# An attention block on one core: group statistics on VectorE in two parts, v's bias placed elsewhere, the weighted sums' banks as two tiles, v's sums in place

## The chip, the cores and the metric

The kernel runs on one core of one Trainium2 chip. The metric is the device time of one execution in microseconds (us). The core has a matrix engine (PE in the profile; its weight loads are listed apart, as PEld), a vector engine (DVE), a scalar engine (ACT), GpSimd (POOL) and a sync engine (SP) that issues transfers. Each engine works through its own queue in order and waits at an instruction until what it needs is done. Matrix products are written to PSUM, which has banks of 128 x 512 fp32 elements; the other tiles are in SBUF, 128 partitions wide.

## The reference

The input is a batch of B = 16 images with C = 512 channels and N = 32 x 32 = 1024 positions, all in fp32. For each image:

```
xn  = group_norm(x, 8 groups of 64 channels) * gamma + beta
q, k, v = qkv_w @ xn + qkv_b              # each 512 x 1024; 4 heads of 128 channels
p   = softmax(q_head^T k_head / sqrt(128))   # 1024 x 1024 per head
o   = p v^T per head, put together to 512 x 1024
y   = x + proj_w @ o + proj_b
```

The channels lie on the partitions, 128 to a tile. So a group of 64 channels is one half of a tile's partitions, two blocks ("quadrants") of 32 partitions. A bias of v adds a constant per channel to v, and, since the weights of a softmax sum to one, the same constant to o.

## The kernel before

The work on an image is a pipeline over "heads". While the attention of image b, head h runs (8 steps, one for each block of 128 keys), other work is put between its matmuls by `plan_head` (L1059):

- head 0: the second half of q and k of image b;
- head 1: the projection of image b-1 (`proj_groups`, L795), and of image b+1 the loads, the statistics (`stats_chunk`, `stats_group`) and the normalisation;
- head 2: the first half of q and k of image b+1;
- head 3: v of image b+1 (`v_groups`, L754).

Image 0's own q, k and v are made before, in an opening part; its v comes from `v_units` (L722). In image 0, head 1 there is no projection yet; there the sums of the projection's weights are made and stored in DRAM (`kept_group`, L943; the sums on DVE at L428 to L442), from which `w<-kept` loads them, and q, k and v's weights likewise.

**Attention.** In each step, `scores` makes two halves s of the scores (L844, PE), ACT makes p = exp(s) (L850), DVE adds the p's into tot (L858), and one step later `weighted_sum` adds p times v into the PSUM tile po (L912, PE). po is one tile of two banks, from a pool with one buffer, so a head's two halves are two banks of one tile. After the last step each half is copied to SBUF (`o`, L919, ACT), and in the next head `divide` multiplies o by the inverse of the sums (L922, DVE).

**Projections.** q, k, v and proj are matrix products by a two-level Strassen scheme (`two_levels`, L521; `strassen`, L470). For each group of outer products, seven inner products (L604, PE) go into two alternating PSUM banks, called x and y; DVE makes the sums of the inputs (L572) and of the products (L628, tensor_add from a bank and an SBUF tile into a row of a tile R), and ACT copies some banks (L484, L626). The last inner product accumulates into bank y, after the L628 of the sum c22 (`v_r<-v_y,v_u` for v) has read y. L677 adds whole R tiles to each other.

**v's end.** For images 1 to 15 `finish` (L758 on) takes two rows a and c of R tiles and adds them into a new tile vt from the pool `ypool` (L766, DVE), transposes vt in blocks of 32 x 32 into a tile vu of the same pool (L769, DVE), and sends vu through DRAM (`vd`) into the final layout with transfers issued by POOL. `ypool` has 4 buffers.

**Statistics.** For image b+1 `stats_chunk` makes sum and sum of squares of each tile of 128 channels on ACT. `stats_group` then takes the averages over the 64 channels of a group by `Norm.group_steps`: a copy (L82), a matmul with an averaging matrix into a bank of the y buffers (pm, L83), three small DVE operations, a copy, a second matmul (pv, L88), an addition of epsilon (L89) and the power -1/2 on POOL (L90). `scale` and `shift` (L76, L100, L102) give two columns per channel, which `normalise` applies on ACT (L109).

**Biases.** In the fast path v gets no bias. Instead `bias_of_v` (L929), planned in image 0's head 1, adds proj_w times v's bias to the projection's bias: 16 matmuls of one column, in four groups of four, and four small additions on DVE. Each matmul here, as all in fp32, is two passes on PE.

**What sets the order.** Each engine's order is made by a scheduler from the order in which the program issues the instructions, from `tc.high_priority(URGENT)`, and from `tc.issue_after(...)`, which puts instructions behind a named other one (the statistics stand behind `added[b-1, 1, n]`, which is the L858 of step n of head 1). Around these points, a changed or removed instruction can change the place of others too.

A second, slower function (`general_path`) is in the program behind a branch, and is not taken with these inputs.

Of the kernel before, what the change touches and what calls it, by code (L numbers as in the profile page):

```python
# [10 lines left out]
F32 = mybir.dt.float32  # L11
# [5 lines left out]
P = 128  # L17
HEADS = 4
# [168 lines left out]
def fast_path(ctx, tc, x, sources, out, consts, flag, dims):  # L187
# [35 lines left out]
    ones = one.tile([BLK, 1], F32, name="ones")  # L223
    xs, xb, vs, qs, ks, os_, ob = {}, {}, {}, {}, {}, {}, {}
# [23 lines left out]
    nc.vector.memset(neghalf, -0.5)  # L248
    for t, src in (
        (gamma_sb, gamma), (beta_sb, beta), (qkb_sb, qk_b), (vb_sb, v_b), (projb_sb, proj_b)  # L250
    ):
        nc.gpsimd.dma_start(t, src)
# [3 lines left out]
    def stats_chunk(b, c):  # L256
        if c == 0:
            mvs[b] = gn.tile([P, NCC, 2], F32, tag="mv", name=f"mv_{b}")
# [4 lines left out]
        nc.scalar.mul(mvs[b][:, c, 0:1], sums[:, 0:1], 1.0 / N)  # L263
        nc.scalar.mul(sums[:, 1:2], sums[:, 0:1], -1.0 / N)
        nc.scalar.activation(
            junk, xs[b, c], AF.Square, bias=sums[:, 1:2], accum_out=sums[:, 2:3]
        )
        nc.scalar.mul(mvs[b][:, c, 1:2], sums[:, 2:3], 1.0 / N)

    def stats_group(b):  # L270


        g = []

        def part(n, first, last):
            if not g:
                g.extend(norm.group_steps(mvs[b]))
            with tc.issue_after(added[b - 1, 1, n].ins), tc.high_priority(URGENT):
                for step in g[first:last]:
                    step()  # L280

        def scale():
            n = 4 if b > 1 else 3
            part(n, 9, 10)
            with tc.issue_after(added[b - 1, 1, n].ins), tc.high_priority(URGENT):
                mu, sc = norm.result
                sh = norm.shift(mu, sc)
            for c in range(NCC):
                scaled[b, c] = sc, sh, c

        return [lambda: part(2, 0, 6), lambda: part(3, 6, 9), scale]
# [462 lines left out]
    def v_groups(b):  # L754
# [3 lines left out]
        def finish(which, h, a, c):  # L758
            pair, half = int(which[1]) - 1, int(which[2]) - 1
            if (b, pair) not in vs:  # L760
# [4 lines left out]
            t = ypool.tile([P, HALF], F32, tag="y", name=f"vt_{b}_{pair}_{h}_{half}")  # L765
            nc.vector.tensor_add(t, a, c)  # L766
# [4 lines left out]
                t.rearrange("p (j q i) -> p j q i", q=n, i=BLK),  # L771
# [135 lines left out]
    def weighted_sum(s, half):  # L907
        b, h, j = where(s)
        if j == 0 and half == 0:
            po[b, h] = ps_o.tile([P, N], F32, tag="o", name=f"po_{b}_{h}")  # L910
        i = ts(half, HALF)
        nc.tensor.matmul(  # L912
            po[b, h][:, i], v_block(b, h, j), ps[s][:, i],
            start=(j == 0), stop=(j == NB - 1),
        )
        if j == NB - 1:
            if (b, h) not in os_:
                os_[b, h] = opool.tile([P, N], F32, tag="o", name=f"o_{b}_{h}")
            last_eviction[b] = nc.scalar.copy(os_[b, h][:, i], po[b, h][:, i])  # L919

    def divide(b, h):
        nc.vector.tensor_mul(os_[b, h], os_[b, h], rinv.pop((b, h)))  # L922

# [4 lines left out]

    def bias_of_v(o):  # L929

        acc = ps_a.tile([P, HALF], F32, tag="y", name=f"pb_{o}")
        half, r = divmod(o, 2)
        for c in range(NCC):
            block = stage["proj"][f"a{half + 1}{c // KC + 1}"]
            nc.tensor.matmul(
                acc[:, 0:1], block[:, ts(r * KC + c % KC, P)], vb_sb[:, c : c + 1],
                start=(c == 0), stop=(c == NCC - 1),
            )
        nc.vector.tensor_add(
            projb_sb[:, o : o + 1], projb_sb[:, o : o + 1], acc[:, 0:1]  # L940
        )
# [117 lines left out]
    def plan_head(b, h):  # L1059
# [9 lines left out]
        elif h == 1:  # L1069
# [4 lines left out]
            else:  # L1074
                plan[0].append(lambda: load_x(b + 1))
                spread(plan, [lambda c=c: stats_chunk(b + 1, c) for c in range(NCC)], 2, 4)
                sums, power, scale = stats_group(b + 1)
                if b == 0:

                    plan[4] += [sums, power, scale]  # L1080
                else:
                    plan[4].insert(0, sums)
                    plan[4].insert((len(plan[4]) + 1) // 2, power)
                    plan[5].insert(0, scale)
# [7 lines left out]
            if b == 0:  # L1092
                for g in range(len(OUTER)):
                    plan[g // 2].append(lambda g=g: kept_group("v", g))
                    plan[NB // 2 - 1 + g].append(lambda g=g: kept_group("proj", g))
                plan[2].append(lambda: stage_blocks("proj"))
                spread(plan, [lambda o=o: bias_of_v(o) for o in range(NCC)], 3, 5)
# [113 lines left out]
    for s in range(steps + 1):  # L1211
# [12 lines left out]
        for half in range(NH2):  # L1224
            if s < steps:
# [4 lines left out]
                if half == 1 and j == 4 and s > NB:  # L1230

                    with tc.issue_after(added[b, h, 4].ins):
                        divide(*where(s - NB)[:2])
            if s > 0:
                weighted_sum(s - 1, half)
# [11 lines left out]
def general_path(ctx, tc, x, sources, out, consts, dims):  # L1247
# [26 lines left out]
    with tc.For_i(0, B, 1) as b:  # L1274
# [16 lines left out]
        for h in range(HEADS):  # L1291
# [9 lines left out]
            for qb in range(NB):  # L1301
# [27 lines left out]
                nc.scalar.copy(o[h][:, ts(qb, P)], acc[:, :P])  # L1329
# [46 lines left out]
```

## Time and profile before

| | |
|---|---|
| Time, median of 3 runs | 3169.58 us (3167.83 to 3171.18) |
| Profiled execution: time / span | 3171.08 us / 3169.30 us |
| Busy: PE, DVE, ACT, POOL | 3156.8 (100%), 2635.8 (83%), 1438.3 (45%), 516.3 (16%) us |
| Chain that ended last | PE 96%, DVE 2%, DMA 1% |
| Granted clock of PE | 1.0 of full speed |
| L83, pm matmuls of 4 columns | 30 passes, 4.3 us |
| L88, pv matmuls of 4 columns | 30 passes, 5.8 us |
| L935, bias of v | 32 passes, 3.8 us |
| L766, v's sums on 512 columns | 90 instructions, 711 ns each |
| L769, v's transposes | 120 instructions, 1131 ns each |
| L922, division | 63 instructions, 1226 ns each |

A line of a group of the profile names the line of the kernel, the engine, the operation, out<-in by the program's names, and the shape; then the busy time in us, the mean of one in ns, and the idle time of the engine ahead of it with what ended it. A line of a timeline has the start in us from the beginning of the span, the duration, and then the same names; "x2" is two instructions in a row, and in brackets stands how long the engine was idle before and for what. Instructions that follow each other overlap by about 0.1 us, so the distance between starts ("step") is shorter than a duration, and for matmuls much shorter. A line of the chain has start, length and what the time was spent in.

### The profile page before, as it was taken

Reading aid. Unit: us, or ns where it says so; the run is one execution under the profiler, and the core shown is the slowest. Engines: PE = TensorE matmul, PEld = TensorE weight load, DVE = VectorE, ACT = ScalarE, POOL = GpSimd, SP = SyncE. Lnnn points to the kernel's source line nnn. Section 1 sums busy time; section 2 is a strip of 40 time slices with the busy share of each in tenths; the row PEclk is TensorE's granted clock in tenths of the full one; section 3 lists DMA queues with packets and bytes.
Section 4 is the critical chain, followed back from the end, with each engine's and each line's share of the span. In section 5 each row is a group of like instructions: output and inputs, shape, how many; then the busy total and the mean of one; then the engine's idle time right before and its main releaser. Section 6 shows DMA issues by size and latency. Waiting matters only on the chain.

```text
span 3169.3 us, 34227 instructions
## 1 busy us (share of the span) xinstructions
PE 3156.8 (100%) x10502; PEld 2188.2 (69%) x10502; DVE 2635.8 (83%) x4642; ACT 1438.3 (45%) x2711; POOL 516.3 (16%) x896
## 2 busy tenths in 40 slices
PE   9999999999999999999999999999999999999999
PEld 7566676677776776767767667677676776766664
DVE  9878879788897888878888787987879978788785
ACT  3535435354353443535435454453534545344333
POOL 0011221111211112211122111222012221122200
PEclk9999999999999999999999999999999999999999
DMA  5554554545545555454554545555455564555531
GB/s 176 186 190 154 187 173 152 173 152 194 168 164 163 155 184 176 167 165 144 193 173 159 170 144 192 167 174 171 144 177 170 176 187 133 178 158 187 180 119 48
DMA packets 210668, 524.83 MB, mean 166 GB/s; under 512 B 32176, under 2 KB 65456, under 8 KB 210480
## 3 DMA queue, kind: packets, MB, share of 16 engines
q1 hardware_dynamic: 133088, 282.39, 28.6%
q0 software_dynamic: 64000, 204.54, 19.3%
q10 hardware_dynamic: 13392, 35.66, 3.5%
q8 instruction: 86, 1.41, 0.2%
q14 instruction: 102, 0.84, 0.1%
HBM read 389.30 MB, written 133.17 MB: 165 GB/s over the span
## 4 chain that ended last, share of the span: by engine, by line
PE 96%; DVE 2%; DMA 1%; issue 0%; SPq 0%; POOL 0%; ACT 0%; ACTq 0%; DVEq 0%
PE s L844 27%; PE po L912 27%; PE qk_x L604 12%; PE qk_y L604 9%; PE pp_x L604 6%; PE v_x L604 6%; PE v_y L604 4%; PE pp_y L604 4%; PE lx L999 0%; DVE qk_t L572 0%; DMA x<-in_x 0%; PE ly L999 0%; DVE tot L858 0%; DVE qk_r L628 0%; DVE qk L712 0%
## 5 line engine op out<-in xcount | busy, mean ns | idle before, releaser
L912 PE MATMUL po<-p,v 128*128 128x512 f32 x2048 | 1049.4, 594 | 0.7 <-ACT p L850 0.7
L850 ACT ACTIVATE p<-s 128x512 f32<-128x512 f32 x1024 | 610.6, 596 | 963.7 <-PE s L844 960.0
L844 PE MATMUL s<-qk,qk 128*128 128x512 f32 x2048 | 1047.4, 593 | 0.3 <-DVE qk L712 0.3
L912 PEld LDWEIGHTS po<-p,v 128*128 128x128 f32 x2048 | 603.6, 302 | 322.7 <-issue 214.5
L858 DVE TENSOR_TENSOR tot<-tot,p 128x1024 f32<-128x1024 f32 x385 | 470.2, 1221 | 158.1 <-ACT p L850 156.1
L844 PEld LDWEIGHTS s<-qk,qk 128*128 128x128 f32 x2048 | 387.7, 190 | 88.6 <-issue 29.9
L604 PEld LDWEIGHTS qk_x<-qk_t,w 128*128 128x128 f32 x1344 | 251.8, 190 | 166.1 <-issue 75.3
L604 PE MATMUL qk_x<-qk_t,w 128*128 128x256 f32 x1344 | 356.3, 382 | 0.1
L484 ACT COPY qk_u<-qk_x 128x512 f32<-128x512 f32 (+1 forms) x256 | 136.2, 532 | 229.6 <-PE qk_x L604 229.6
L777 POOL DMA_DIRECT2D vd<-vu x120 | 66.6, 556 | 902.9 <-DVE vu L769 899.5
L628 DVE TENSOR_TENSOR qk_r<-qk_y,qk_u 128x512 f32<-128x512 f32 (+1 forms) x256 | 158.1, 618 | 34.7 <-ACT qk_u L484 21.5
L578 POOL DMA_DIRECT2D kept_t<-qk_t x240 | 129.3, 540 | 278.5 <-DVE qk_t L572 212.0
L604 PEld LDWEIGHTS pp_x<-pp_t,w_proj 128*128 128x128 f32 x630 | 117.2, 190 | 74.7 <-issue 32.3
L628 DVE TENSOR_TENSOR v_r<-v_y,v_u 128x512 f32<-128x512 f32 (+1 forms) x120 | 76.6, 638 | 110.5 <-ACT v_u L484 80.3
L604 PE MATMUL pp_x<-pp_t,w_proj 128*128 128x256 f32 x630 | 167.8, 383 | 0.0
L782 POOL DMA_DIRECT2D v<-vd x240 | 140.5, 592 | 166.6 <-DMA vd<-vu 63.3
L604 PE MATMUL v_x<-v_t,w_v 128*128 128x256 f32 x630 | 166.6, 381 | 0.0
L828 POOL DMA_DIRECT2D out_y<-y x120 | 65.9, 550 | 603.3 <-DVE y L827 601.5
L604 PEld LDWEIGHTS v_x<-v_t,w_v 128*128 128x128 f32 x630 | 118.4, 190 | 55.3 <-issue 19.1
L604 PE MATMUL qk_y<-x,w 128*128 128x256 f32 x512 | 142.2, 379 | 1.5 <-DVE qk_r L628 1.5
L769 DVE STREAM_TRANSPOSE vu<-vt 128x512 f32<-128x512 f32 x120 | 135.7, 1131 | 4.5 <-DMA vd<-vu 4.4
L712 DVE SCALAR_TENSOR_TENSOR qk<-qk_r,qkb_sb,qk_r 128x512 f32<-128x512 f32 x192 | 137.7, 744 | 1.6
(203 smaller groups left out, 4420.0 us busy)
## 6 DMA issues: line engine op xcount, KB each, us to landing
w<-kept SPq DMA_DIRECT2D x90, 512.0 KB, 3.7
kept_t<-qk_t POOLq DMA_DIRECT2D x180, 256.0 KB, 3.5
v_t<-kept_t SPq DMA_DIRECT2D x180, 256.0 KB, 2.9
w<-kept SPq DMA_DIRECT2D x90, 384.0 KB, 3.3
rinv<-row ACTq DMA_DIRECT2D x63, 512.0 KB, 5.0
x<-in_x POOLq DMA_DIRECT2D x60, 512.0 KB, 4.6
vd<-vu POOLq DMA_DIRECT2D x120, 256.0 KB, 3.0
v<-vd POOLq DMA_DIRECT2D x240, 128.0 KB, 4.2
```

Source lines behind the costliest of these rows:

```text
L484: nc.scalar.copy(t[n][:, :width], t["x"][:, :width])
L578: nc.gpsimd.dma_start(t, to)
L604: nc.tensor.matmul(acc[:, ts(i, Q)], have["w"][t][:, i, slot, :], inner(i, bn), start=(first and i == 0), stop=True, skip_group_check=True,)
L628: nc.vector.tensor_add(dst, view(a), view(c))
L712: nc.vector.scalar_tensor_tensor(st[b, h][:, ts(half, HALF)], a, qkb_sb[:, i : i + 1], c, ALU.add, ALU.add)
L769: nc.vector.transpose(u.rearrange("p (q i j) -> p j q i", q=n, i=BLK), t.rearrange("p (j q i) -> p j q i", q=n, i=BLK),)
L777: nc.gpsimd.dma_start(rows[which][ts(h, P), :], u)
L782: nc.gpsimd.dma_start(vs[b, pair][ts(q, BLK), half].rearrange("m h (k i) j -> m (h k) (i j)", k=n), rows[which].rearrange("(k m) (q e) -> ...
L844: nc.tensor.matmul(sc, ks[b, h][:, ts(j, P)], qs[b, h][:, ts(half, HALF)], start=True, stop=True)
L850: exps[s] = nc.scalar.activation(ps[s][:, ts(half, HALF)], sc, AF.Exp, scale=SCALE)
L858: added[b, h, j] = nc.vector.tensor_add(tot[b, h][:, i], tot[b, h][:, i], ps[s][:, i])
L912: nc.tensor.matmul(po[b, h][:, i], v_block(b, h, j), ps[s][:, i], start=(j == 0), stop=(j == NB - 1),)
```

## The change

It has four parts.

1. **Statistics of images 1 to 15.** The sums of a tile go as columns into a permanent table of 128 x 2 x 32 (the columns not used are zero, from a memset on POOL at the start). `gather` transposes the table in blocks of 32 x 32 on DVE, so that a chunk's 32 means lie along a row of its own quadrant, copies each quadrant's rows beside those of the other quadrant of the same group (four copies), and takes mean and variance over the 64 entries by one `bn_aggr`; then epsilon is added, and POOL takes the power of one column. `scale` transposes back, and multiplies by gamma. Both matmuls and the small operations around them go. `gather` stands behind step 3 and `scale` behind step 4 (3 in image 0) of head 1; the parts before stood behind 2, 3 and 4. Image 0's own statistics stay as they were.
2. **v's bias.** `bias_of_v` with its matmuls goes. In image 0 the bias is added to o by an ACT operation on 128 x 1024, placed behind the exp of step 6 of the next head; in all later images it is added in `finish`.
3. **v's sums in place.** In `finish`, one DVE operation computes (a + bias) + c and writes it over c; the transpose reads c. The tile vt is gone.
4. **Banks of the weighted sums.** po is two tiles of one bank each.

The general path adds v's bias where it evicts o.

```diff
     def stats_chunk(b, c):
...
+        mean, spread_ = (
+            (mvs[b][:, c, 0:1], mvs[b][:, c, 1:2]) if b == 0
+            else (table[:, 0, c : c + 1], table[:, 1, c : c + 1])
+        )
...
         nc.scalar.activation(
-            junk, xs[b, c], AF.Square, bias=sums[:, 1:2], accum_out=sums[:, 2:3]
+            junk, xs[b, c], AF.Square, bias=sums[:, 1:2],
+            accum_out=sums[:, 2:3] if b == 0 else spread_,
         )
-        nc.scalar.mul(mvs[b][:, c, 1:2], sums[:, 2:3], 1.0 / N)
+        if b == 0:
+            nc.scalar.mul(spread_, sums[:, 2:3], 1.0 / N)
 
     def stats_group(b):
...
+        def gather():
+            t["all"] = lpool.tile([P, N], F32, tag="tt", name=f"groups_{b}")
+            rows = t["all"][:, : 6 * BLK].rearrange("p (s j) -> p s j", s=3)
+            both = t["both"] = t["all"][:, 6 * BLK : 6 * BLK + 2]
+            ve = t["all"][:, 6 * BLK + 2 : 6 * BLK + 3]
+            v.memset(rows[:, 0, :], float(N))
+            v.transpose(rows[:, 1:3, :BLK], table)
+            for q in range(quads):
+                v.tensor_copy(rows[ts(q, BLK), 1:3, BLK:], rows[ts(q ^ 1, BLK), 1:3, :BLK])
+            v.bn_aggr(both, rows.rearrange("p s j -> p j s"))
+            v.tensor_scalar_add(ve, both[:, 1:2], EPS)
+            nc.gpsimd.tensor_tensor(both[:, 1:2], ve, neghalf[:, 0:1], ALU.pow)
 
         def scale():
-            n = 4 if b > 1 else 3
-            part(n, 9, 10)
-            with tc.issue_after(added[b - 1, 1, n].ins), tc.high_priority(URGENT):
-                mu, sc = norm.result
-                sh = norm.shift(mu, sc)
+            back = t["all"][:, 8 * BLK : 10 * BLK].rearrange("p (s j) -> p s j", s=2)
+            v.transpose(back, t["both"].unsqueeze(2).to_broadcast([P, 2, BLK]))
+            sc = gn.tile([P, NCC], F32, tag="sc", name="sc")
+            v.tensor_mul(sc, back[:, 1, k], gamma_sb)
+            sh = norm.shift(back[:, 0, k], sc)
             for c in range(NCC):
                 scaled[b, c] = sc, sh, c
 
-        return [lambda: part(2, 0, 6), lambda: part(3, 6, 9), scale]
+        def part(n, step):
+            with tc.issue_after(added[b - 1, 1, n].ins), tc.high_priority(URGENT):
+                step()
+
+        return [lambda: part(3, gather), lambda: part(4 if b > 1 else 3, scale)]
...
             n = P // BLK
-            t = ypool.tile([P, HALF], F32, tag="y", name=f"vt_{b}_{pair}_{h}_{half}")
-            nc.vector.tensor_add(t, a, c)
+            i = 2 * pair + h
+            nc.vector.scalar_tensor_tensor(c, a, vb_sb[:, i : i + 1], c, ALU.add, ALU.add)
 
             u = ypool.tile([P, HALF], F32, tag="y", name=f"vu_{b}_{pair}_{h}_{half}")
             nc.vector.transpose(
                 u.rearrange("p (q i j) -> p j q i", q=n, i=BLK),
-                t.rearrange("p (j q i) -> p j q i", q=n, i=BLK),
+                c.rearrange("p (j q i) -> p j q i", q=n, i=BLK),
             )
...
-        if j == 0 and half == 0:
-            po[b, h] = ps_o.tile([P, N], F32, tag="o", name=f"po_{b}_{h}")
+        if j == 0:
+            po[half] = ps_o.tile([P, HALF], F32, tag=f"o{half}", name=f"po_{b}_{h}_{half}")
...
+    def bias_of_v(b, h):
+        nc.scalar.activation(os_[b, h], os_[b, h], AF.Identity, bias=vb_sb[:, h : h + 1])
...
-    def bias_of_v(o):
-
-        acc = ps_a.tile([P, HALF], F32, tag="y", name=f"pb_{o}")
-        half, r = divmod(o, 2)
-        for c in range(NCC):
-            block = stage["proj"][f"a{half + 1}{c // KC + 1}"]
-            nc.tensor.matmul(
-                acc[:, 0:1], block[:, ts(r * KC + c % KC, P)], vb_sb[:, c : c + 1],
-                start=(c == 0), stop=(c == NCC - 1),
-            )
-        nc.vector.tensor_add(
-            projb_sb[:, o : o + 1], projb_sb[:, o : o + 1], acc[:, 0:1]
-        )
...
-                spread(plan, [lambda o=o: bias_of_v(o) for o in range(NCC)], 3, 5)
...
+                if half == 1 and j == 6 and NB < s < (HEADS + 1) * NB:
+
+                    with tc.issue_after(exps[s].ins):
+                        bias_of_v(*where(s - NB)[:2])
```

In the built program this moves instructions on DVE as well. In `v_groups` of every image from 1 on, the first sum in place of a pair now stands ahead of the L858 that precedes it, transposes follow each other in twos, and the division L922 stands ahead of the L628 (`v_r<-v_y,v_u`) behind which it stood before; at the next L628 of this kind that has 256 columns one more transpose is ahead. In `proj_groups` one L858 now stands ahead of a late L628. PE's order is the same but for the matmuls that are gone and one pair of po that moves behind ten matmuls of qk in image 0.

More of the change, by code (lines that the diff above doesn't have):

```diff
@@ L223, in fast_path @@
     ones = one.tile([BLK, 1], F32, name="ones")
+    table = one.tile([P, 2, BLK], F32, name="table")
     xs, xb, vs, qs, ks, os_, ob = {}, {}, {}, {}, {}, {}, {}
@@ L248, in fast_path @@
     nc.vector.memset(neghalf, -0.5)
+    nc.gpsimd.memset(table, 0.0)
     for t, src in (
@@ L256, in stats_chunk @@
     def stats_chunk(b, c):
-        if c == 0:
-            mvs[b] = gn.tile([P, NCC, 2], F32, tag="mv", name=f"mv_{b}")
+        mean, spread_ = (
+            (mvs[b][:, c, 0:1], mvs[b][:, c, 1:2]) if b == 0
+            else (table[:, 0, c : c + 1], table[:, 1, c : c + 1])
+        )
         junk = lpool.tile([P, N], F32, tag="tt", name=f"junk_{b}_{c}")
@@ L262, in stats_chunk @@
         nc.scalar.activation(junk, xs[b, c], AF.Identity, accum_out=sums[:, 0:1])
-        nc.scalar.mul(mvs[b][:, c, 0:1], sums[:, 0:1], 1.0 / N)
+        nc.scalar.mul(mean, sums[:, 0:1], 1.0 / N)
         nc.scalar.mul(sums[:, 1:2], sums[:, 0:1], -1.0 / N)
         nc.scalar.activation(
-            junk, xs[b, c], AF.Square, bias=sums[:, 1:2], accum_out=sums[:, 2:3]
-        )
-        nc.scalar.mul(mvs[b][:, c, 1:2], sums[:, 2:3], 1.0 / N)
+            junk, xs[b, c], AF.Square, bias=sums[:, 1:2],
+            accum_out=sums[:, 2:3] if b == 0 else spread_,
+        )
@@ L270, in stats_group @@
+        if b == 0:
+            nc.scalar.mul(spread_, sums[:, 2:3], 1.0 / N)
     def stats_group(b):
[L273 to L277, printed above, removed]
-            with tc.issue_after(added[b - 1, 1, n].ins), tc.high_priority(URGENT):
-                for step in g[first:last]:
-                    step()
-        def scale():
-            n = 4 if b > 1 else 3
-            part(n, 9, 10)
-            with tc.issue_after(added[b - 1, 1, n].ins), tc.high_priority(URGENT):
-                mu, sc = norm.result
-                sh = norm.shift(mu, sc)
+        v = nc.vector
@@ new lines, in stats_group @@
+        quads = P // BLK
+        k = slice(0, NCC)
+        t = {}
+        def gather():
[10 more added lines that the diff above has]
+            nc.gpsimd.tensor_tensor(both[:, 1:2], ve, neghalf[:, 0:1], ALU.pow)
@@ L908, in weighted_sum @@
         b, h, j = where(s)
-        if j == 0 and half == 0:
-            po[b, h] = ps_o.tile([P, N], F32, tag="o", name=f"po_{b}_{h}")
+        if j == 0:
+            po[half] = ps_o.tile([P, HALF], F32, tag=f"o{half}", name=f"po_{b}_{h}_{half}")
         i = ts(half, HALF)
         nc.tensor.matmul(
-            po[b, h][:, i], v_block(b, h, j), ps[s][:, i],
+            po[half], v_block(b, h, j), ps[s][:, i],
             start=(j == 0), stop=(j == NB - 1),
@@ L918, in weighted_sum @@
                 os_[b, h] = opool.tile([P, N], F32, tag="o", name=f"o_{b}_{h}")
-            last_eviction[b] = nc.scalar.copy(os_[b, h][:, i], po[b, h][:, i])
+            last_eviction[b] = nc.scalar.copy(os_[b, h][:, i], po[half])
     def divide(b, h):
         nc.vector.tensor_mul(os_[b, h], os_[b, h], rinv.pop((b, h)))
+    def bias_of_v(b, h):
+        nc.scalar.activation(os_[b, h], os_[b, h], AF.Identity, bias=vb_sb[:, h : h + 1])
     def spread(plan, units, first, last):
@@ L1076, in plan_head @@
                 spread(plan, [lambda c=c: stats_chunk(b + 1, c) for c in range(NCC)], 2, 4)
-                sums, power, scale = stats_group(b + 1)
+                gather, scale = stats_group(b + 1)
                 if b == 0:
-                    plan[4] += [sums, power, scale]
+                    plan[4] += [gather, scale]
                 else:
-                    plan[4].insert(0, sums)
-                    plan[4].insert((len(plan[4]) + 1) // 2, power)
+                    plan[4].insert(0, gather)
                     plan[5].insert(0, scale)
@@ L1328, in general_path @@
                     )
-                nc.scalar.copy(o[h][:, ts(qb, P)], acc[:, :P])
+                nc.scalar.activation(
+                    o[h][:, ts(qb, P)], acc[:, :P], AF.Identity, bias=vb_sb[:, h : h + 1]
+                )
         for i in range(NCC):
```

## The prediction

> **What bounds the kernel now.** I read the page's shares first, then the chain that ended last, the groups, PE's timeline where the change takes matmuls away, and VectorE's (DVE's) where it puts work in. Shares, chain, and the groups that the change touches, from the page and the groups by form:
>
> ```profile
> PE 3156.8 (100%) x10502; PEld 2188.2 (69%) x10502; DVE 2635.8 (83%) x4642; ACT 1438.3 (45%) x2711; POOL 516.3 (16%) x896
> ...
> PE 96%; DVE 2%; DMA 1%; issue 0%; SPq 0%; POOL 0%; ACT 0%; ACTq 0%; DVEq 0%
> ...
> L769 DVE STREAM_TRANSPOSE vu<-vt 128x512 f32<-128x512 f32 x120 | 135.7, 1131 | 4.5 <-DMA vd<-vu 4.4
> ...
> L766 DVE TENSOR_TENSOR vt<-v_r,v_r 128x512 f32<-128x512 f32 x90 | 64.0, 711 | 0.5
> ```
>
> PE is the bound: its passes start back to back (0.43 us for 512 columns, 0.215 for 256). So a matmul removed is worth its own slot, work on another engine is free while PE does not wait for it, and every wait of PE counts in full. DVE at 83% is full for stretches, and there its order decides. PE's timeline of one image (start, duration, instructions):
>
> ```profile
> 1095.12 0.28 PE L83 MATMUL pm<-mean,avg 128*128 128x4 f32 x2
> 1095.26 1.11 PE L604 MATMUL pp_x<-ot,w_proj 128*128 128x256 f32 x4
> 1096.21 1.02 PE L844 MATMUL s<-qk,qk 128*128 128x512 f32 x2
> ...
> 1101.81 0.59 PE L604 MATMUL pp_y<-ot,w_proj 128*128 128x256 f32 x2
> 1102.33 0.39 PE L88 MATMUL pv<-vv,avg 128*128 128x4 f32 x2
> 1102.57 1.10 PE L844 MATMUL s<-qk,qk 128*128 128x512 f32 x2
> 1103.52 1.02 PE L912 MATMUL po<-p,v 128*128 128x512 f32 x2
> ```
>
> From 1095.12 to 1096.21 there are 1.09 us where four 256-column passes need 0.86: pm costs 0.23. From 1101.81 to 1103.52 there are 1.71 where two passes of 256 and two of 512 need 1.29: pv costs 0.42.
>
> DVE and PE where v is made, two stretches:
>
> ```profile
> 1008.06 1.23 DVE L677 TENSOR_TENSOR v_r<-v_r,v_r 128x1024 f32<-128x1024 f32 x1
> 1009.19 1.23 DVE L858 TENSOR_TENSOR tot<-tot,p 128x1024 f32<-128x1024 f32 x1
> 1010.31 0.70 DVE L628 TENSOR_TENSOR v_r<-v_y,v_u 128x512 f32<-128x512 f32 x1
> 1010.91 1.23 DVE L922 TENSOR_TENSOR o<-o,rinv 128x1024 f32<-128x1024 f32 x1
> 1011.07 0.83 PEld L604 LDWEIGHTS v_y<-xt,w_v 128*128 128x128 f32 x4 [0.34 <-DVE v_r L628]
> ...
> 1019.39 0.43 DVE L628 TENSOR_TENSOR v_r<-v_y,v_u 128x256 f32<-128x256 f32 x1
> 1019.72 1.09 DVE L769 STREAM_TRANSPOSE vu<-vt 128x512 f32<-128x512 f32 x1
> 1019.87 0.30 PEld L604 LDWEIGHTS v_y<-x,w_v 128*128 128x128 f32 x2 [0.52 <-DVE v_r L628]
> ```
>
> DVE's queue has no gap from 1003.50 to 1022. Strassen's last product goes into PE's bank y only after L628 has read it, and PE's weight load starts 50 ns after L628's end at both places. There is no slack left.
>
> **The change part by part.** The profiled execution took 3171.08 us (span 3169.30 and 1.78 around it), 1.50 above the median of 3169.58; the sum is made against 3171.08.
>
> *Statistics, images 2 to 15.* pm and pv go: 0.23 + 0.42 = 0.65, of which I take 0.64 (other images read 0.64): 14 x 0.64 = **-9.0**. What replaces them is DVE work: a memset, a transpose, four copies, an aggregation, an add. No row shows this aggregation; from below, L52 (128x12) took 0.21, from above 192 values at L766's 1.39 ns per column plus 0.15 make 0.42. The small ones lie between their starting distance of 0.08 and L875's 0.19, so the gather is 0.8 to 1.8 us, and I take 1.4. It stands behind the L858 that ends at 1099.1. Behind it DVE is idle for 1.19 us until L628 at 1101.58 waits for PE, and one small L89 (0.12) goes: covered, and PE reads behind that L628 only at 1105.24, 3 us after its end. The power (L90) sees one column instead of four and starts earlier, so shift ends in time. Of a step moved: one L858 (step 1.13) now stands ahead of the L628 of 1120.23, whose reader on PE starts at 1121.71; that L628 starts 0.70 later (1.13, less 0.40 that DVE has gained by then) and about 0.1 is left. Priced at 0, with 0 to 0.3 per image for the range. ACT loses one tiny multiply per chunk.
>
> *Image 0 and image 1's statistics.* 32 bias matmuls (L935) go, 32 x 0.112 = 3.6 us between starts, and pm and pv of image 1, 2.0 with their wait. But this stretch of the chain is not PE's:
>
> ```profile
> 123.49 5.50 DMA st_a<-in_proj_wT
> 129.11 0.69 DVE st_s L387
> ...
> 149.82 3.96 DMA kept_proj<-w_proj
> 153.79 5.28 DMA w<-kept
> 159.21 1.97 PE qk_x L604 x8
> ```
>
> DVE idles until the load at 129.11, is then full until the last sums of w_proj at 149.8, and PE's qk_x waits for the store and the load back. The matmuls lie beside that. In front of the last sums one small sum more (0.33) and the gather with scale stand in place of the old small operations, which included a wait of 0.9 for the power. Bounds: -5.6 if all of PE's work reaches the end, +1.5 if the gather comes wholly on top; I take **+0.3**, being nearest to the chain's rows. Image 0's bias on ACT is 4 operations like L985 (1.14 us each) behind an exp; the divide that they read ended at 133.8, 176.5, 228.8 and 274.4, ahead of each; ACT is 45% busy: 0.
>
> *v's sums in place, the table of images 1 to 15.* The add (step 0.60) becomes an operation with a bias column, like L712 and L824 (0.74, step 0.66). It does not wait for a buffer any more, so it and its transpose (step 0.95) move forward on DVE. Up to the first L628 above (1010.31): one add was done earlier in an idle stretch (-0.60), one is dearer (+0.06), and the divide L922 (step 1.13) now stands ahead: +0.57 or so. Up to the second (1019.39): the same number of adds, four times 0.05 to 0.06 dearer, and one transpose more (0.95): +1.15. PE waits for both: 0.5 at the first, and 1.15 in all at the second, since DVE's queue has no gap in which PE's delay would be lost. 15 x 1.15 = **+17.2**. After 1022 DVE has 1 to 7 us of slack at PE's next reads, so no more follows.
>
> *Banks as two tiles.* A half's first matmul no longer waits for the eviction of the other half. From PE's timeline of the last image, then ACT's:
>
> ```profile
> 3083.66 1.23 PE L912 MATMUL po<-p,v 128*128 128x512 f32 x2
> 3084.72 1.02 PE L844 MATMUL s<-qk,qk 128*128 128x512 f32 x2
> ...
> 3084.93 0.58 ACT L919 COPY o<-po 128x512 f32<-128x512 f32 x1 [0.47 <-PE po L912]
> ```
>
> 1.06 between starts where 0.86 would do: 0.2, five times in that image. **-1.0** (from 0 to -1.2).
>
> *A wait of this execution.* In image 14 a transpose waited for a buffer that a DMA was reading, and PE for the DVE behind it (the lists of waits of DVE and PE):
>
> ```profile
> DVE vu L769 <- DMA vd<-vu: 2.3, 2, 1.5
> ...
> PE qk_y L604 <- DVE qk_r L628: 1.5, 1, 1.5
> ```
>
> The sums leave that pool, so its buffers come free sooner: **-1.7** against this execution (PE stood from 2997.26 to 2998.91). Late next there is nothing.
>
> Sum: 3171.1 - 9.0 + 0.3 + 17.2 - 1.0 - 1.7 = **3176.9**, say 3177, which is 0.23% above the median before.
>
> **Rivals.** A change of 0.2% (6.3 us, bounds 3163.2 and 3175.9) is about what a measurement of this kernel tells from none.
>
> *R1, the other side: DVE reaches both L628 in time.* Place: the 7 us before 1010.31. If operations that now follow each other as pairs (add and add, transpose and transpose) start 0.57 us closer together than their rows, the first wait is gone, at 1.15 both. For it: the add no longer comes right before its own transpose. Against: steps in pairs and alone read the same in L572 and L858. Time 3176.9 - 17.2 = 3159.7.
>
> *R2: only the first wait comes.* The transpose pulled forward finds its buffer still held and falls behind the second L628. Then 15 x 0.5 = 7.5: 3167.2. For it: DVE's waits for vd above. Against: they came in one image.
>
> *R3: the gather is longer than its cover.* Then PE waits at the read of 1121.71, where only 0.1 is left, and at the next ones. With 1 us more than I take, 14 x 0.9 = 12.6: 3189.5. For it: L873 starts 0.20 behind L872, as long as it lasts, where the two are in different partitions, while other small operations start 0.08 apart; four copies at 0.20 add 0.5. Against: 1.19 us of idle time would still take that.
> [...]
>
> *R4: image 0's matmuls reach the end* (DVE's chain shortens with them): 3176.9 - 5.9 = 3171.0.
>
> **How the numbers follow.** Forecast 0.52, spread over 3171 to 3182 by the bounds above (0.39 above 3175.9, 0.13 below); R1 0.18; R2 0.10 (a third of it, with a gain besides, below 3163.2); R3 0.12; R4 0.08 (0.02 above 3175.9). Faster: 0.18 + 0.03 = 0.21. Slower: 0.39 + 0.12 + 0.02 = 0.53. Same: 0.13 + 0.07 + 0.06 = 0.26. Range: down to R1 (3159), up to half of R3 (3187); the forecast's own is 3171 to 3182.
>
> **What would show it.** In the profile after: no L83 or L88 behind image 0, PE 0.64 us shorter in head 1; DVE at the place of 1010 with L922 ahead of L628, and PE's v_y waiting for L628 some 0.5 us there and 0.6 more at the second; an image period of 195.8 + 1.15 - 0.64 = 196.3 us; qk_x of image 0 still behind the w<-kept load near 159; copies of quadrants 0.08 or 0.20 apart. The prediction is wrong if the v_y waits are missing (R1, R2), if pp_y waits in head 1 (R3), or if image 0 ends some 5 us earlier (R4).

## The result and the profile after

The changed kernel took 3181.46 us (median of 6 runs, 3179.49 to 3183.10), the kernel before 3169.08 (6 runs, 3167.81 to 3171.18). The ratio is 1.0039, with a 95% interval from 1.0027 to 1.0051: 12.4 us slower. The forecast was 3177 (3159 to 3187), slower; it came out slower, by 12.4 us where it had 7.8 over the median before.

In the new line numbers L622 is the inner product (L604 before), L646 the sum that reads bank y (L628), L784 the new sum in place, L787 the transpose (L769), L876 the sum of the p's (L858), L940 the division (L922), L590 the sums of inputs (L572) and L335 the sum of x (L317).

The page of the profile after: busy times, and the chain by engine.

```profile
PE 3155.4 (99%) x10410; PEld 2176.6 (68%) x10410; DVE 2666.3 (84%) x4683; ACT 1438.3 (45%) x2655; POOL 495.4 (16%) x897
...
PE 86%; DVE 11%; issue 2%; DMA 1%; SPq 0%; ACT 0%; DVEq 0%; ACTq 0%; POOL 0%; POOLq 0%
```

PE has 92 passes less and 1.4 us less to do, and yet the span is 11.9 us longer. The chain, which ran over PE for 96%, now leaves it for 11% and runs over DVE. The list of waits of PE's weight loads names where (total us, times, longest), first before, then after:

```profile
PEld v_y L604 <- DVE v_r L628: 13.9, 30, 0.8
...
PEld pp_y L604 <- DVE pp_r L628: 0.2, 1, 0.2
```

```profile
PEld v_y L622 <- DVE v_r L646: 31.7, 30, 1.3
...
PEld pp_y L622 <- DVE pp_r L646: 16.9, 29, 0.8
```

The weight loads run ahead of the matmuls, so only a part of such a wait is time that PE loses: at the first place below v_y's weight loads wait 0.96 us and PE loses 0.42, at the second 1.14 and 0.6. That part is read from the distance between the starts of passes. The first place where v is made: one line of before, from which the distance below is counted, then DVE's timeline after and PE's of the same image (this is the place that stood at 1003.50 to 1011.28 before):

```profile
1003.50 0.69 DVE L766 TENSOR_TENSOR vt<-v_r,v_r 128x512 f32<-128x512 f32 x1
```

```profile
1008.56 0.75 DVE L784 SCALAR_TENSOR_TENSOR v_r<-v_r,vb_sb,v_r 128x512 f32<-128x512 f32 x1
1009.23 1.22 DVE L695 TENSOR_TENSOR v_r<-v_r,v_r 128x1024 f32<-128x1024 f32 x1
1010.36 2.09 DVE L787 STREAM_TRANSPOSE vu<-v_r 128x512 f32<-128x512 f32 x2
1012.24 0.47 DVE L590 TENSOR_TENSOR qk_t<-x 128x256 f32<-128x256 f32 x1
1012.56 1.26 DVE L695 TENSOR_TENSOR v_r<-v_r,v_r 128x1024 f32<-128x1024 f32 x1
1013.69 1.27 DVE L876 TENSOR_TENSOR tot<-tot,p 128x1024 f32<-128x1024 f32 x1
1014.82 1.27 DVE L940 TENSOR_TENSOR o<-o,rinv 128x1024 f32<-128x1024 f32 x1
1015.96 0.73 DVE L646 TENSOR_TENSOR v_r<-v_y,v_u 128x512 f32<-128x512 f32 x1
```

```profile
1015.46 1.03 PE L930 MATMUL po<-p,v 128*128 128x512 f32 x2
1016.74 0.92 PE L622 MATMUL v_y<-xt,w_v 128*128 128x256 f32 x3 [0.25 <-DVE v_r L646]
```

The division stands ahead of L646, as the order had said. The two passes of po begin at 1015.46 and would take 0.86, so v_y could begin at 1016.32 and begins at 1016.74: 0.42 lost, and another 0.105 between its first two passes. From L784's start to L646's it is 7.40 us, where before 6.81 lay between 1003.50 and 1010.31: 0.59 more. The second place, DVE and PE after:

```profile
1024.63 0.71 DVE L784 SCALAR_TENSOR_TENSOR v_r<-v_r,vb_sb 128x512 f32<-128x512 f32 x1
...
1025.56 0.44 DVE L646 TENSOR_TENSOR v_r<-v_y,v_u 128x256 f32<-128x256 f32 x1
...
1024.59 1.03 PE L930 MATMUL po<-p,v 128*128 128x512 f32 x2
1026.06 0.70 PE L622 MATMUL v_y<-x,w_v 128*128 128x256 f32 x2 [0.43 <-DVE v_r L646]
```

From po to v_y there are 1.47 us where 0.86 would do: PE loses 0.6. Over all 15 images the lengthened distances at both places sum to 16.6 us more than before.

The statistics, DVE in head 1 of one image, and the end of that head, where pp_y waits. First the end of the head before (DVE, then PE), then after:

```profile
1120.23 0.42 DVE L628 TENSOR_TENSOR pp_r<-pp_y,pp_u 128x256 f32<-128x256 f32 x1
...
1120.83 1.04 PE L912 MATMUL po<-p,v 128*128 128x512 f32 x2
1121.71 0.59 PE L604 MATMUL pp_y<-o,w_proj 128*128 128x256 f32 x2
1122.14 1.02 PE L844 MATMUL s<-qk,qk 128*128 128x512 f32 x2
```

```profile
1104.97 0.11 DVE L288 MEMSET groups<- 128x64 f32 x1
1104.99 0.19 DVE L289 STREAM_TRANSPOSE groups<-table 128x64 f32<-128x64 f32 x1
1105.11 0.38 DVE L590 TENSOR_TENSOR pp_t<-ot,pp_t 128x256 f32<-128x256 f32 x1
1105.50 0.78 DVE L291 COPY groups<-groups 32x64 f32<-32x64 f32 x4
1106.31 0.42 DVE L590 TENSOR_TENSOR pp_t<-ot,pp_t 128x256 f32<-128x256 f32 x1
1106.66 1.01 DVE L292 BATCH_NORM_AGGREGATE groups<-groups 128x2 f32<-128x192 f32 x1
...
1125.86 1.21 DVE L876 TENSOR_TENSOR tot<-tot,p 128x1024 f32<-128x1024 f32 x1
1126.99 0.41 DVE L646 TENSOR_TENSOR pp_r<-pp_y,pp_u 128x256 f32<-128x256 f32 x1
```

```profile
1126.38 1.04 PE L930 MATMUL po<-p,v 128*128 128x512 f32 x2
1127.46 0.70 PE L622 MATMUL pp_y<-o,w_proj 128*128 128x256 f32 x2
1128.00 1.02 PE L862 MATMUL s<-qk,qk 128*128 128x512 f32 x2
```

The gather takes 2.0 us of DVE without the two L590 between its parts, half of it the aggregation. Behind it PE waits at the end of the head: from 1126.38 to 1128.00 there are 1.62 us, 0.31 more than the 1.31 from 1120.83 to 1122.14 before. This is the place of the L876 that now stands ahead of L646. L646 started 0.60 ahead of the first pass of po before, and starts 0.61 behind it now: 1.21 later.

In the middle of the head PE does not wait for DVE, but ACT does. In the lists of waits, ACT's normalisation (L109) waited for shift (L102) 2 times before, 0.6 us in total, and waits 16 times after, 12.1 us in total: 0.5 us in each image, and 4.4 in image 0's head 1. ACT works without a gap from there to its copy pp_p of PE's bank, whose end PE's weight load of pp_x waits for, and the passes there (from 1121.57) lose 0.07 us per image, 1.0 in all.

### The profile page after: what moved, and what is told of

Its sections match the earlier page's. It is cut to its first block, busy times and chain, and to the rows that moved or that the text cites. A ratio compares the mean times of both kernels' runs of the same rounds, so it can differ in the third digit from the quotient of the medians.

```text
span 3181.2 us, 34098 instructions
## 1 busy us (share of the span) xinstructions
PE 3155.4 (99%) x10410; PEld 2176.6 (68%) x10410; DVE 2666.3 (84%) x4683; ACT 1438.3 (45%) x2655; POOL 495.4 (16%) x897
## 4 chain that ended last, share of the span: by engine, by line
PE 86%; DVE 11%; issue 2%; DMA 1%; SPq 0%; ACT 0%; DVEq 0%; ACTq 0%; POOL 0%; POOLq 0%
PE s L862 24%; PE po L930 24%; PE qk_x L622 12%; PE qk_y L622 9%; PE pp_x L622 5%; PE pp_y L622 4%; PE v_x L622 4%; PE v_y L622 3%; DVE vu L787 2%; DVE v_r L646 1%; DVE tot L876 1%; DVE v_r L695 1%; DVE qk_t L590 1%; DVE v_r L784 1%; DVE o L940 1%
## 5 line engine op out<-in xcount | busy, mean ns | idle before, releaser
L876 DVE TENSOR_TENSOR tot<-tot,p 128x1024 f32<-128x1024 f32 x385 | 471.5, 1225 | 120.0 <-ACT p L868 118.2
L622 PEld LDWEIGHTS qk_x<-qk_t,w 128*128 128x128 f32 x1344 | 252.1, 190 | 166.4 <-issue 75.3
L622 PE MATMUL qk_x<-qk_t,w 128*128 128x256 f32 x1344 | 357.2, 382 | 0.1
L646 DVE TENSOR_TENSOR qk_r<-qk_y,qk_u 128x512 f32<-128x512 f32 (+1 forms) x256 | 157.9, 617 | 36.7 <-ACT qk_u L502 20.9
L646 DVE TENSOR_TENSOR v_r<-v_y,v_u 128x512 f32<-128x512 f32 (+1 forms) x120 | 76.2, 635 | 110.6 <-ACT v_u L502 80.3
L622 PE MATMUL pp_x<-pp_t,w_proj 128*128 128x256 f32 x630 | 168.8, 385 | 0.0
L622 PEld LDWEIGHTS pp_x<-pp_t,w_proj 128*128 128x128 f32 x630 | 116.0, 190 | 76.9 <-issue 25.6
L622 PE MATMUL v_x<-v_t,w_v 128*128 128x256 f32 x630 | 166.6, 381 | 0.0
L622 PEld LDWEIGHTS v_x<-v_t,w_v 128*128 128x128 f32 x630 | 118.4, 190 | 55.3 <-issue 19.1
L622 PE MATMUL qk_y<-x,w 128*128 128x256 f32 x512 | 142.5, 380 | 0.0
L502 ACT COPY v_u<-v_x 128x512 f32<-128x512 f32 (+1 forms) x124 | 66.2, 534 | 157.2 <-PE v_x L622 131.5
```

The source lines that it names most:

```text
L502: nc.scalar.copy(t[n][:, :width], t["x"][:, :width])
L622: nc.tensor.matmul(acc[:, ts(i, Q)], have["w"][t][:, i, slot, :], inner(i, bn), start=(first and i == 0), stop=True, skip_group_check=True,)
L646: nc.vector.tensor_add(dst, view(a), view(c))
L876: added[b, h, j] = nc.vector.tensor_add(tot[b, h][:, i], tot[b, h][:, i], ps[s][:, i])
```

## The experiments

The theory (A in all of them): PE is the bound, it waits for DVE at three L628 of an image, and how long it waits is the sum of the rows that stand ahead of that L628 in DVE's queue. So the parts' costs add up, and each can be undone by the order alone. The main rival: the operations themselves cost (the sum in place, the bias column, the gather's length). All differences below are of medians against the kernel before in the same series.

**The parts one by one.** Each is the kernel before with one part of the change.

Part 1, the statistics: the diff of `stats_chunk`, `stats_group` and their place in `plan_head`, as above.

> Before with part 1 alone (table, gather and scale for images 1 to 15). Theory A (PE's slots and DVE's order decide): pm and pv of images 2 to 15 are worth 14 x 0.64 = -9.0 us; the L858 that now stands ahead of the late pp L628 makes PE's pp_y wait 0.3 us per image, +4.3; image 0 gives 0 to +2. Together -5 to -3 us against before, no v_y waits. Rival B (the gather, measured at about 2.3 us in image 0, is longer than its cover): PE waits in the middle of head 1, about 1 us per image, and the time is +5 us or more.

Measured: 3166.24 against 3168.96 us, ratio 0.9990 (0.9981 to 0.9999): -2.7. That is 0.3 short of theory A's range, which had left out the 1.0 us of pp_x; the rival's +5 is out. pp_y loses the same 0.31 us per image as in the full change, and v_y waits no more than before:

```profile
1120.91 1.04 PE L930 MATMUL po<-p,v 128*128 128x512 f32 x2
1121.99 0.70 PE L622 MATMUL pp_y<-o,w_proj 128*128 128x256 f32 x2
1122.53 0.59 PE L862 MATMUL s<-qk,qk 128*128 128x512 f32 x1
```

Part 3, the sum in place, without the bias:

```diff
-            t = ypool.tile([P, HALF], F32, tag="y", name=f"vt_{b}_{pair}_{h}_{half}")
-            nc.vector.tensor_add(t, a, c)
+            nc.vector.tensor_add(c, a, c)
...
-                t.rearrange("p (j q i) -> p j q i", q=n, i=BLK),
+                c.rearrange("p (j q i) -> p j q i", q=n, i=BLK),
```

> Before with the in-place sum alone: tensor_add over c, no vt, no bias in it, the 16 bias matmuls kept. Theory A (the place in DVE's queue decides): L628 v_y,v_u at two places 0.5 and 0.95 us later, PE waits 0.95 us per image, 15 x 0.95 = +14 us, less up to 1.7 for the wait for a buffer in image 14: +12 to +14 us. Rival B (what costs is the operation with the bias column, or the end of the bias matmuls): within 2 us of before.

Measured: 3182.63 against 3168.96 us, 1.0044 (1.0030 to 1.0058): +13.7. This part alone costs more than the whole change does. The instructions themselves are no dearer: in the groups the sum in place took 705 ns a piece (711 into vt before) and the transpose 1140 (1131).

Part 2, the bias at v (into vt, as before) and on image 0's output:

```diff
-            nc.vector.tensor_add(t, a, c)
+            i = 2 * pair + h
+            nc.vector.scalar_tensor_tensor(t, a, vb_sb[:, i : i + 1], c, ALU.add, ALU.add)
```

with `bias_of_v` exchanged as in the change.

> Before with the bias at v alone: (a + bias) + c into vt as before, image 0's bias on ACT, the 16 bias matmuls gone. Theory A: DVE's order is before's, four operations 0.05 to 0.06 us dearer stand ahead of an L628 without slack, 15 x 0.2 = +3 us; the matmuls' 3.6 us in image 0 lie beside a chain of DVE and DMA and give nothing, and the longer wait of PE there can bring a stretch of lower clock, 0 to +2. Together +3 to +5 us. Rival B (the matmuls' time reaches the end): -3.6 + 3 = -0.6 us.

Measured: 3170.82 against 3168.96 us, 1.0006 (0.9997 to 1.0015): +1.9, below theory A's +3 to +5. The direction can't be told from no change. The distances between passes lengthen by 0.14 us per image at the second v_y; times 15 that is +2.1. The 3.6 us of bias matmuls did not come out as a gain: the first matmul of v of image 1 started at 192.64 us in this trace and at 193.37 before, 0.7 earlier. So rival B's -0.6 is the worse fit, though the interval does not exclude it.

Part 4, the two tiles of one bank each:

> Before with two tiles of one bank for the weighted sums alone. Theory A: the five waits of 0.2 us for the eviction of the other half in the last image go, -1.0 us, and nothing else changes: -0.5 to -1.2 us. Rival B (ACT's eviction or the next wait takes their place): 0.

Measured: 3167.96 against 3168.96 us, 0.9996 (0.9987 to 1.0005): -1.0, too small for its interval. The trace shows it plainly: the waits of po's weight loads for `o` (L919), 3.2 us in the last image before, are not in the list any more, and what the distances between passes have over their back-to-back distance falls by 1.0 us behind 3000 us of the span.

The four together: -2.7 + 13.7 + 1.9 - 1.0 = +11.9, and the whole change was +12.4. Within the intervals the parts add up; no part is seen to hide another.

**The whole change without the sum in place.**

```diff
-            nc.vector.scalar_tensor_tensor(c, a, vb_sb[:, i : i + 1], c, ALU.add, ALU.add)
+            t = ypool.tile([P, HALF], F32, tag="y", name=f"vt_{b}_{pair}_{h}_{half}")
+            nc.vector.scalar_tensor_tensor(t, a, vb_sb[:, i : i + 1], c, ALU.add, ALU.add)
...
-                c.rearrange("p (j q i) -> p j q i", q=n, i=BLK),
+                t.rearrange("p (j q i) -> p j q i", q=n, i=BLK),
```

> The changed kernel, with v's biased sum written to a tile vt of the pool again and transposed from there. DVE's order in the v phase is then that of before. Theory A (the order costs): PE's v_y waits fall from 1.13 us per image to about 0.2, 15 x 0.9 = -14 us against the changed kernel: 3167 to 3168 us, the sum of the other three parts alone. Rival B (operation with the bias column, in place or not): no more than 2 us below 3181.

Measured: 3166.47 against 3168.35 us, 0.9995 (0.9986 to 1.0004): -1.9, where the other three parts sum to -1.8. So the sum in place is what makes the change slow, and it can't be the bias column, which is still there.

**In place, but in another order.** The two kernels so far change the operation and the order together. Here both are the in-place kernel, and only the order differs: from the fifth sum on, sums and transposes are issued behind the L628 of the second place.

```diff
+                        read = nc.vector.tensor_add(dst, view(a), view(c))
+                        if site == "v" and g == len(OUTER) - 1 and which == "c22":
+                            last_read[b] = read
...
+            with tc.issue_after(last_read[b].ins) if count[0] > 4 else nullcontext():
                 nc.vector.tensor_add(c, a, c)
```

(the transposes likewise; in the last group the finishing steps wait until four products are issued)

> Before with the in-place sum alone, as one_v_in_place, but from the fifth sum of an image on the sums and transposes are issued behind the L628 of the second place. At that L628 one sum less (0.60) and one L572 more (0.33) then stand ahead, so it is 0.27 us earlier: 0.68 us late in place of 0.95; the first place is unchanged. Theory A (PE's wait is the sum of the rows ahead of that L628): the first wait stays near 0.47, the second falls from 0.47 to 0.2, 15 x 0.27 = -4 us against the in-place sum alone, 3178 to 3179 us. Rival B (the operation in place itself costs, wherever it stands): 3182 to 3183 us.

Measured: 3178.59 against 3168.75 us, 1.0031 (1.0019 to 1.0044): +9.8, and 3.8 less than the sum in place alone. The two timelines of DVE at that place, first of the sum in place alone, then of this kernel:

```profile
1019.88 2.06 DVE L768 STREAM_TRANSPOSE vu<-v_r 128x512 f32<-128x512 f32 x2
1021.76 0.70 DVE L765 TENSOR_TENSOR v_r<-v_r 128x512 f32<-128x512 f32 x1
1022.36 0.43 DVE L628 TENSOR_TENSOR v_r<-v_y,v_p 128x256 f32<-128x256 f32 x1
1022.69 0.43 DVE L628 TENSOR_TENSOR v_r<-v_y,v_u 128x256 f32<-128x256 f32 x1
```

```profile
1019.72 2.06 DVE L775 STREAM_TRANSPOSE vu<-v_r 128x512 f32<-128x512 f32 x2
1021.58 0.45 DVE L573 TENSOR_TENSOR qk_t<-x,qk_t 128x256 f32<-128x256 f32 x1
1021.93 0.44 DVE L629 TENSOR_TENSOR v_r<-v_y,v_p 128x256 f32<-128x256 f32 x1
1022.25 0.44 DVE L629 TENSOR_TENSOR v_r<-v_y,v_u 128x256 f32<-128x256 f32 x1
```

The last line of each is the sum that PE's v_y waits for. A sum of 0.60 is exchanged for one of 0.33, and PE's second wait falls from 0.47 to 0.21 us while the first stays (0.37 and 0.36). The number and the kind of operations are the same: it is their place. This undoes 3.8 of the 13.7 us by order alone. That the rest is order too is read from the rows ahead of both places, from the instructions being no dearer (705 against 711 ns), and from the run with a tile vt, where before's order and before's time came back together.

**The division back behind the first L628.**

```diff
-                if half == 1 and j == 4 and s > NB:
+                if half == 1 and j == (5 if h == 3 else 4) and s > NB:
```

(and the `issue_after` with it). This kernel leaves something out: the sums that the last image's projection takes of this head's o (at 3124.9 us) stand ahead of the division (3142.1), so this division is left out of them. Where v is made, it does the same work as the changed kernel.

> The changed kernel with the division of head 2 (L922) planned one step later, in head 3 only. DVE's order then has L628 v_y,v_u ahead of the division at the first place (0.1 us late in place of 0.57), and at the second place the division, one transpose more, one sum less and one L572 more ahead: 0.85 to 0.9 us late. Theory A (DVE's queue has no gap between both places, so the second lateness contains the first): the first wait all but goes, the second grows to about 0.9, and the sum falls only by 0.2 to 0.3 us per image, -3 to -4 us: 3177 to 3178 us. Rival B (the two waits are independent): the first wait's 0.53 us per image goes and the second stays at 0.6, -8 us: 3173 to 3174 us.

Measured: 3180.03 against 3168.35 us, 1.0034 (1.0022 to 1.0046): +11.7, only 0.7 below the whole change's +12.4. The waits of PE tell why:

```profile
PE v_y L622 <- DVE v_r L646: 12.4, 15, 0.8
```

Fifteen waits in place of thirty: the first is gone altogether, and the second has grown from 0.6 to 1.0 us. Rival B's -8 is out: the second lateness holds the first. The size was off, -0.7 in the medians (-1.0 by the distances between passes at v_y) for -3 to -4; 0.85 to 0.9 was expected at the second place and 1.0 came, which was not followed further.

**The sum that stands ahead of pp_y.** Part 1 alone, with the L858 of step 6 of head 1 issued behind the projection's work of that step:

```diff
+        elif h == 1 and b > 0 and j == 6:
+            late[s] = lambda: late_add(s, i)
...
             run(units[half * n : (half + 1) * n])
+            if half == 1 and s in late:
+                late.pop(s)()
```

> Before with part 1 alone, and the L858 of step 6 of head 1 issued behind the projection's work of that step, so that it stands behind the late L628 again (one x sum L317 of 0.6 us is still ahead of it). Theory A: the pp_y wait of 0.3 us per image is due to that L858: it goes, -4.3 us against part 1 alone, 3161.5 to 3162.5 us. Rival B (the gather's own length delays DVE up to there): the wait stays, 3166 us.

Measured: 3161.34 against 3168.35 us, 0.9976 (0.9966 to 0.9986): -7.0, where part 1 alone gave -2.7: 4.3 us, as 14 times 0.31 says. PE's timeline at that place:

```profile
1117.73 1.04 PE L938 MATMUL po<-p,v 128*128 128x512 f32 x2
...
1118.61 0.59 PE L622 MATMUL pp_y<-o,w_proj 128*128 128x256 f32 x2
1119.04 1.02 PE L862 MATMUL s<-qk,qk 128*128 128x512 f32 x2
```

1.31 from po to s, as before, so the wait is gone. On DVE, the same place:

```profile
1117.21 0.68 DVE L335 TENSOR_TENSOR x<-x 128x512 f32<-128x512 f32 x1
1117.81 0.41 DVE L646 TENSOR_TENSOR pp_r<-pp_y,pp_u 128x256 f32<-128x256 f32 x1
```

L646 starts 0.08 behind po here, 0.68 later than before, and nothing is lost; with the L858 ahead in place of this sum of x it starts 0.61 behind. So the gather alone does not make the wait, and rival B is out. That its length has no part in it is not shown: it is as long in both kernels, no run shortens it, and at both places DVE is late by 0.08 beyond the step of the sum that stands ahead (1.13 and 0.60).

**Versions to beat both.** Parts 1 and 4 with that order, without parts 2 and 3; in the first, image 1's statistics also stay on the two matmuls.

> Parts 1 and 4 without parts 2 and 3, the L858 of step 6 of head 1 issued behind the projection's work, and image 1's statistics made as before with two matmuls. By the parts: -9.0 (pm and pv of 14 images), -1.0 (banks), no v_y wait beyond before's, no pp_y wait, image 0 as before: 3158.5 to 3160 us, faster than both kernels. If the gather's DVE time still cost PE something in head 1, 3163 us or more.

> Parts 1 and 4 without 2 and 3, the L858 of step 6 of head 1 behind the projection's work, image 1's statistics on DVE like the others. By the runs so far: 3161.3 for parts 1 with that L858, less 1.0 for the banks: 3160 to 3160.7 us. If image 0 again loses 1.5 us to a longer wait for w<-kept, as where image 1 kept its matmuls, 3161.5 us.

Measured: 3161.45 against 3168.35 us, 0.9975 (0.9965 to 0.9985), and 3161.58 against 3168.71 us, 0.9978 (0.9969 to 0.9987). Both are 7 us faster than the kernel before and about 20 faster than the change, but no better than part 1 alone with that order (-7.0), and above the times expected (3158.5 to 3160, and 3160 to 3160.7, or 3161.5 for the second with a longer wait in image 0). The 1.0 us of the banks is there in the last image of both traces. In the profiled executions it gets lost in image 0, where the first has a wait of 3.0 us and the second a stretch of low clock (granted clock 0.61 from 160 to 164 us). But the second's profiled execution took 3162.99 us, 1.4 above its median, so where its median lost the 1.0 us is open.

**Image 0's low clock.** In the profile after, PE's granted clock falls in image 0 to 0.50 for 3.41 us (160.25 to 163.66), behind the second of two idle times of PE (the distance between two starts, less the pass): 3.0 us from 137.9 (PE s <- ACT p; ACT's next exp stands behind a normalisation that waits for shift) and 3.4 us from 155.9 (w<-kept). Busy times by stretch (start:end, length, then PE, weight loads, DVE, ACT, POOL, and the clock ahead of DMA share and GB/s), after:

```profile
136.00:141.00 5.00, 2.19 (x6) 0.68 (x5) 4.54 (x13) 2.16 (x4) 0.53 (x1) 1.00 0.50 183
...
155.00:160.00 5.00, 1.78 (x7) 0.90 (x6) 4.92 (x16) 0.59 (x1) 1.08 (x2) 1.00 0.87 232
160.00:164.00 4.00, 4.00 (x13) 3.21 (x12) 0.69 (x3) 1.67 (x3) 0.00 (x0) 0.57 0.59 236
```

Eight passes of 256 columns took 0.43 instead of 0.215 us: 1.7 us. Two kernels filled one of the idle times each with matmuls whose result is not used.

```diff
+            if s == 2 * NB + 1 and half == 1:
+                warm(14, "warm_gap")
```

> The changed kernel with 14 added matmuls of 128 columns (their result is not used; they only keep PE busy, about 3 us) in image 0 ahead of the 3.4 us in which PE waits for w<-kept. Theory A (the stretch of granted clock 0.57 behind that wait comes from PE's own idle time): no low clock between 160 and 164 us, qk_x still begins near 159.3 since the load sets it, 1.7 us gained: 3179.5 to 3180 us. Rival B (the low clock comes from something else in this place, the load's traffic or the steps themselves): it stays, 3181 us or more.

> The changed kernel with 12 added matmuls of 128 columns (result not used, about 2.6 us) in image 0's head 1, beside the earlier idle time of 3.0 us (PE s <- ACT p at 137.5 to 140.9); the later wait of 3.4 us at 155.5 stays. Theory A (a wait of over 3 us alone is enough for the low clock): eight passes at half speed behind 160 us stay, 3181 to 3182 us. Rival B (it takes both idle times within some 20 us): the low clock is gone, 1.7 us gained, 3179.5 to 3180 us.

(the other: 12 at step 6 of head 1, into a bank of the y buffers). Measured: 3185.47 and 3185.55 against 3168.71 us, 1.0051 (1.0038 to 1.0065) and 1.0053 (1.0039 to 1.0066). Both are 4 us slower than the change. The added matmuls moved some matmuls of the scores behind the idle times, so their own 3 us probably came on top, and the times say nothing on the clock. The first one's stretches do:

```profile
141.00:145.00 4.00, 4.00 (x6) 1.76 (x7) 4.00 (x11) 3.35 (x6) 0.00 (x0) 0.59 0.58 229
155.00:160.00 5.00, 2.74 (x11) 1.60 (x10) 4.92 (x13) 0.94 (x2) 1.08 (x2) 1.00 0.79 238
160.00:164.00 4.00, 4.00 (x18) 3.17 (x17) 2.03 (x7) 1.17 (x2) 0.00 (x0) 1.00 0.59 228
```

Behind the wait that was filled, of which 2.4 us were left idle, there is no low clock, but there is one behind the first idle time, which in the change had none. The other kernel has it behind both (idle 2.5 and 2.4 us): 0.57 from 141 to 145 us, and 0.83 from 156 to 160 and 0.74 from 160 to 164. Neither theory A nor rival B of these two runs holds as it stood.

## Why the prediction was right, and where its sum was off

*PE bounds, and its distances are the price.* Right. The parts' prices, read from starts of passes, add up to the whole.

*Statistics of images 2 to 15, -9.0.* Right for the matmuls: the distances around pm and pv that are gone sum to 8.9 us. *The gather, 1.4 us, from 0.8 to 1.8.* Too low: 2.0, above the upper bound. The term that failed is the aggregation (0.21 to 0.42 bounded, 1.01 measured), and the copies, which were priced between 0.08 and 0.19 and start 0.20 apart. At the L628 behind it the cover named was enough: the 1.19 us of idle time is used up (DVE has no gap from 1104.97 to that sum), and the rest lies within the 3 us until PE reads. But "so shift ends in time" did not hold: ACT waits 0.5 us for shift in most images, and 1.0 us of PE's time goes at pp_x, also in the run that put the L858 back.

*The L858 moved ahead of the late L628, priced at 0, up to 0.3 per image.* This is the step that was mis-sized: it took 0.31 us per image, 4.3 in all, the upper end of the price, and the run that put the L858 back gave 4.3. The prediction reached the right place, but had L628 only 0.70 later, 1.13 less 0.40 that DVE gains by then. It came 1.21 later: DVE gained nothing. At 0.68 later, in the run that put the L858 back, PE lost nothing, so by the forecast's own 0.70 the price of 0 would have been right. The gather's 0.6 us above the forecast is of the size of the gain that is missing; that it is the reason is argued, since no run shortens the gather. Of the 0.31, 0.105 is that the first two passes behind the late load start 0.320 apart in place of 0.215.

*R3, the gather longer than its cover.* The prediction named pp_y waiting in head 1 as a sign that it is wrong. pp_y does wait, at the read that R3 names, for a third of R3's price (4.3 for 12.6), and a gather longer than forecast came with it. So this sign came true, and the total stayed in the range because the wait was short.

*v's sums in place, +17.2.* Right: 16.6 by the distances. The place (division ahead of the first L628, one transpose more ahead of the second), the sizes (0.5, and 1.1 in all) and that the second contains the first were all borne out. Of the two causes the order has nearly all: +13.7 for the sum in place alone, against +1.9 for the dearer operation and the bias at v.

*Banks, -1.0.* Right by the trace, -1.0. *The wait in image 14, -1.7.* Right: PE's 1.66 us there are gone. But it belonged to this execution: the median before is 2.0 us below the profiled one, so against the median this term was no gain, and the sum should have been read with that in mind. Nor is it shown to come from the sums leaving the pool: the traces of parts 2 and 4 alone, which keep vt in the pool, do not have the wait either.

*Image 0, +0.3, from -5.6 to +1.5.* The mechanism held: qk_x began at 159.33 where it had begun at 159.21, and R4's 5.9 us did not come. Then the low clock added 1.7, which the prediction had not thought of. The first matmul of v of image 1 started at 195.19 us, against 193.37 before: 1.8 later, which is the 0.1 of qk_x and the 1.7 of the low clock. Two other kernels with the same work in image 0 (part 1 alone, and that with the L858 put back) had 195.34 and 193.37, without low clock, so 2 us lie within what differs from one execution to the next here. How much of the 1.8 is the change's was not settled.

The sum against the profiled execution: forecast +5.8, measured +11.9 (3182.96 against 3171.08). The difference is pp_y's 4.3, the 1.0 of pp_x in the same head, and 1.5 in image 0, less 0.6 that v cost less. So the mechanism that decided the direction, v's sums, was right in place and size, and what was missed is the statistics part. R1, R2 and R4 did not come.

## What to carry to other kernels

Where one engine runs back to back, price a change by what it puts ahead of the few instructions that this engine waits for without slack, and not by its operations. Taking a buffer away here made DVE's work no longer (705 against 711 ns for a sum), but let it run early, ahead of an instruction with zero slack: with the tile from the small pool, DVE's order was the one that the matmuls needed. And a slack of 0.1 us that is worked out with a term known only to within 1 us is no slack: either put the order back, as a few lines did here for 4.3 us, or carry the term's range through to the wait.

## What the runs showed of the hardware that was not expected

- The aggregation over 64 triples (192 values per partition) took 1.01 us, and over 12 values 0.21 before: (1.01 - 0.21) / 180 = 4.4 ns for each value, an estimate from two points, where a sum of two tiles takes 1.39 ns per column (711 ns for 512). The longer one reads its triples with a stride, so how much the stride adds is open.
- Copies of 32 partitions that go from one quadrant to another (the four of the gather, 0.78 us together) start 0.20 us apart at a duration of 0.18 to 0.19, while other small operations start 0.08 apart: they do not overlap. Why was not shown.
- PE's granted clock fell to 0.50 for 3.41 us in the change, from 160.25 to 163.66 us, behind an idle time of 3.4 us, and was 1.00 from 141 to 145 us, behind one of 3.0. The length of the idle time alone does not decide it. By the lists of waits, which have 0.16 us less in the change than the distance between starts, the second version of parts 1 and 4 has a clock of 0.61 from 160 to 164 us with waits of qk_x of 1.9 and 0.8 us, and the first has 1.00 there with one of 2.9. A wait of 2.3 us has 0.57 behind it in the kernel whose first idle time was filled (141 to 145 us), and 1.00 in the one whose second was (160 to 164 us). What decides it was not shown.
